# A DRAM scratch array stored chunk by chunk instead of partition by partition

## The chip, the cores and the metric

One core of one Trainium2 chip runs the whole program in one launch. The metric is the device time of that launch in microseconds (us). The unchanged kernel took 11381.7 us as the median of three runs (11377.09 to 11388.17).

## What is computed

64 images of 256x256 pass through a four-layer Fourier network with 32 channels, whose output is one value a pixel. Each row of the output image is a token of width 256; 77 text tokens are appended, and a transformer layer (attention and a routed feed-forward) follows. All is in float32.

```python
v = h @ p_w + p_b                                  # 3 -> 32 channels
for i in range(4):
    x1 = fourier_layer(v, W1, W2)                  # 24 x 12 modes kept
    x2 = einsum('bcxy,cd->bdxy', v, w_w[i]) + w_b[i]
    v = batch_norm(x1 + x2)                        # statistics over all images
    if i < 3: v = relu(v)
out = einsum('bcxy,cu->bxyu', v, q_w) + q_b        # 32 -> 1 channel
h = concatenate([out, txt], axis=1)                # 256 + 77 tokens
h = h + attention(layernorm(h))
h = h + routed_ffn(layernorm(h))
```

The batch norm needs the statistics of all 64 images before any of them can enter the next layer. So the activations of a layer, 64 images x 32 channels x 256 x 256 in float32, are 512 MB, and they lie in DRAM (HBM) between the layers.

## The kernel before

An image's activations are 8 MB and are worked on as 8 chunks, numbered t, of 1 MB each: 128 partitions x 8 rows x 256 values. A chunk's SBUF tile has 8 KB in each partition.

The list `vd` holds two DRAM tiles of 8 MB for each image, one set read and the other written by a layer, in turns. They are declared at line 183. Before the change a tile's dimensions are partition, chunk, row, value.

`layer(i, ...)` (line 526) runs three times, for i = 0, 1, 2. For each chunk of each image:

- `ld` (line 632, in layers 1 and 2 alone) loads the previous layer's chunk into a tile `vin`, of which the pool has four. It does so in two DMAs of 512 KB, each of 4 rows in all partitions (line 636).
- `pre` (line 656) makes the new values in PSUM with TensorE: the inverse Fourier part from `y`, and in layers 1 and 2 the 32x32 channel mix of `vin` (line 673).
- `evA` and `evB` (lines 685 and 687) apply the relu and write the tile `vo`, of which there are four, by ScalarE or VectorE.
- `st` (line 691) stores `vo` to DRAM in two DMAs of 512 KB (line 694).
- `turn` (VectorE transpose, line 699), `prod` and `sq` (lines 710 and 721: the mix for the next layer's variance, squared by ScalarE), `y` (line 732: the forward Fourier part) use the same `vo`.

Layer 0 has no `ld`: it builds its input from the raw image, which GpSimd loads. The order of all steps within an image is written out by hand in two strings (`ORDER`, one for layer 0 and one for layers 1 and 2), in which `@1` or `@2` means the step belongs to one or two images later. So instructions stand on every engine in that fixed order.

All loads and stores of activations are issued by SyncE (SP), in program order, on one DMA queue. The DMAs of this queue use eight completion semaphores in rotation, and the program has each of them wait for the DMA eight before it, besides the wait for its data or its buffer. For instance, the first half of a store waits for the eighth DMA back and for ScalarE.

The mixing of modes (`mix`, line 410) runs between the layers. It needs all images' spectra and works on no activation.

The last layer's activation is never stored. `image_rows(b)` (line 942) reads the third layer's chunks again as tiles `ch`, 1 MB in one DMA each (line 962), and contracts the 32 channels to one with TensorE (line 964). There are seven `ch` buffers. `attention` and `feed_forward` then work on the tokens, and the loads run up to two images ahead of them.

Of the kernel before, what the change touches and what calls it, by code (L numbers as in the profile page):

```python
# [9 lines left out]
F32 = mybir.dt.float32  # L10
# [6 lines left out]
S = 256  # L17
# [136 lines left out]
def tile_fno_fusion_transformer(ctx: ExitStack, tc: tile.TileContext, a, cst_d, grid_d, out):  # L154
    nc = tc.nc
    x = a["x"].rearrange("b x y o -> b x (y o)")
    B = x.shape[0]
# [4 lines left out]
    dram = ctx.enter_context(tc.tile_pool(name="dram", bufs=1, space=DRAM))  # L162
# [17 lines left out]
    epsc = const.tile([128, 1], F32, name="epsc")  # L180
    nc.vector.memset(epsc, EPS)

    vd = [dram.tile([128, 8, 8, S], F32, name=f"v{b}_{n}") for n in range(2) for b in range(B)]
    vd = [vd[:B], vd[B:]]
    mix_d = [dram.tile([B, 2, KX, 32 * C], F32, name=f"mix{i}") for i in range(L)]
    xh_d = [dram.tile([128, B, 144], F32, name=f"xh{i}") for i in range(1, L)]
# [3 lines left out]
    def evict(dst, src, act_every=3):  # L190

        flip[0] += 1
        if act_every and flip[0] % act_every == 0:
            nc.scalar.copy(dst, src)
        else:
            nc.vector.tensor_copy(dst, src)
# [329 lines left out]
    def layer(i, st, src, dst, acc):  # L526
# [7 lines left out]
        with ExitStack() as cx:  # L534
# [64 lines left out]
            y_, t32, vin, vo, half_, zts = {}, {}, {}, {}, {}, {}  # L599
# [32 lines left out]
            def ld(b, t, e):  # L632
                vin[b, t] = ip.tile([128, 8, S], F32, name="vin")
                for n in range(2):
                    rows = slice(4 * n, 4 * n + 4)
                    nc.sync.dma_start(vin[b, t][:, rows], src[b][:, t, rows])

            def sp(b, h, e):
                ps = take(("sp", b, h), 1)[0]
# [51 lines left out]
            def st_(b, t, e):  # L691
                for n in range(2):
                    rows = slice(4 * n, 4 * n + 4)
                    nc.sync.dma_start(dst[b][:, t, rows], vo[b, t][:, rows])

            def turn(b, t, e):
                if (b, t // 2) not in t32:
# [84 lines left out]
            def xs(b, n, e):  # L782
                nc.sync.dma_start(xh_d[i][:, b, :], xos.pop(b).rearrange("p g k -> p (g k)"))

            run = dict(
                am=am, lx=lx, ld=ld, sp=sp, spT=spT, pre=pre, evA=ev(0), evB=ev(1), st=st_, turn=turn,
                prod=prod, sqA=sq(0), sqB=sq(1), y=y, half=half, zt0=zt(0), zt1=zt(1), x=x_, xo=xo, xs=xs,
            )
            steps = []
            for word in ORDER[min(i, 1)].split():  # L790
                word, _, late = word.partition("@")
                word, _, e = word.partition(".")
                name = word if word in run else word.rstrip("0123456789")
# [50 lines left out]
    src = vd[L % 2]  # L844
# [87 lines left out]
    rows = [128, 128, TXT]  # L932
# [6 lines left out]
    def psum():  # L939
        return pp.tile([128, 512], F32, name="pp")  # L940

    def image_rows(b):
        am = ap_.tile([2 * KX, 32 * C], F32, name="am")
        nc.sync.dma_start(am, mix_d[L - 1][b].rearrange("p k c -> (p k) c"))
        tmp = am.rearrange("p (o k) -> p o k", k=32)
        nc.vector.tensor_tensor(
            tmp, tmp, qrow[0:2 * KX].to_broadcast([2 * KX, C, 32]), ALU.mult
        )
        a1 = ap_.tile([2 * KX, 32], F32, name="a1")
        nc.vector.reduce_sum(a1, tmp.rearrange("p o k -> p k o"), axis=AX.X)  # L950
        ps = psum()
        nc.tensor.matmul(ps[0:32, 0:S], lhsT=a1, rhs=EXT[0:2 * KX], start=True, stop=True)
        y1 = ap_.tile([32, 2, 128], F32, name="y1")
        evict(y1.rearrange("k t p -> k (t p)"), ps[0:32, 0:S], 2)
        hp = pb_.tile([128, 2, S], F32, name="hp")
        for t in range(2):
            nc.tensor.matmul(  # L957
                hp[:, t, :], lhsT=y1[:, t, :], rhs=T4[0:32], start=t == 0, stop=False, skip_group_check=True
            )
        for t in range(8):  # L960
            ch = inp.tile([128, 4, 2, S], F32, name="ch")
            nc.sync.dma_start(ch.rearrange("p g r y -> p (g r) y"), src[b][:, t])
            for g in range(4):
                nc.tensor.matmul(  # L964
                    hp[32 * g:32 * g + 32], lhsT=win[:, 7 - t:39 - t], rhs=ch[:, g], start=False, stop=t == 7,
                    skip_group_check=True,
                )
        h = tp.tile([128, 3, D], F32, name="h")
        nc.scalar.activation(h[:, 0:2, :], hp, AF.Identity, bias=hbias, scale=1.0)  # L969
        nc.sync.dma_start(h[0:TXT, 2, :], a["txt"][b])  # L970
        return h
# [131 lines left out]
    def feed_forward(b, h1, z, fw, place):  # L1103
# [65 lines left out]
        nc.gpsimd.dma_start(out[b, S:TOK], o[0:TXT, 2, :])  # L1169

    hs = {n: image_rows(n) for n in range(min(2, B))}
    done = attention(hs.pop(0))
    done += select(done[1])
    for b in range(B):
        now = done
        if b + 2 < B:
            hs[b + 2] = image_rows(b + 2)
        if b + 1 < B:
            done = attention(hs.pop(b + 1))
        feed_forward(b, *now)  # L1180
        if b + 1 < B:
            done += select(done[1])
# [33 lines left out]
```

## Time and profile before

| what | value |
|---|---|
| median of three runs | 11381.7 us |
| the profiled execution's own time | 11393.82 us |
| its span, first to last instruction | 11392.0 us |
| TensorE (PE) busy | 10594.2 us |
| VectorE (DVE) busy | 8460.5 us |
| ScalarE (ACT) busy | 6496.0 us |
| GpSimd (POOL) busy | 1477.9 us |
| read from HBM / written to it | 1761.87 MB / 1696.92 MB |

The profiled execution lies 12.1 us above the median, 0.1%. A page of this profile shows the busy share of each engine in 40 slices of the span, the share of the 16 DMA engines in use, and the bytes that they moved. By the times at which lines run, the program has these stages: first transform and mix (to about 300 us), layer 0 (to about 2300 us), mix (to about 2680 us), layer 1 (to about 5450 us), mix (to about 5800 us), layer 2 (to about 8600 us), mix and weight preparation (to about 8790 us), then contraction, attention and feed-forward of the 64 images.

A matmul's end in this profile is modelled and matmuls overlap, so a high PE share doesn't say that PE is at its peak. The share of the DMA engines is the sum of the durations of their packets over 16 times the stretch. The trace also has every single packet, with its start, duration and size.

### The profile page before, as it was taken

The numbers are of one execution on the slowest core, as the hardware profiler recorded it, in microseconds if no ns is written. First come the engines' busy times: TensorE is split into PE (matmuls) and PEld (weight loads), VectorE is DVE, ScalarE is ACT, GpSimd is POOL, SyncE is SP. The second block draws the span as 40 slices with busy tenths as digits, with TensorE's granted clock in tenths as the row PEclk, the third lists the DMA queues.
The fourth block names the chain that finished last, engine by engine and source line by source line (L and its number), as shares of the span: only waits on it lengthen the run. The fifth ranks groups of instructions, "written<-read, shape, count | busy, mean of one in ns | idle before, by whom it ended". The sixth has DMA issues, their size and how long they took to land. (4 is left out here: it accounts for less than half of the span.)

```text
span 11392.0 us, 408517 instructions
## 1 busy us (share of the span) xinstructions
PE 10594.2 (93%) x182038; PEld 5729.6 (50%) x182038; DVE 8460.5 (74%) x10405; ACT 6496.0 (57%) x10697; POOL 1477.9 (13%) x2243
## 2 busy tenths in 40 slices
PE   6999999997999999999699999999995999999998
PEld 3555555543444444444344444444443666666666
DVE  5888888886777777777677777777775666666665
ACT  5777777775656655665556566565653333333333
POOL 0111111110000000000100000000001333333333
PEclk7999999998999999999899999999997999999999
DMA  7776676769999999999899999999998555555553
GB/s 233 248 248 244 247 250 246 248 238 326 378 383 376 383 379 375 376 380 380 296 374 383 379 383 380 377 373 371 382 376 279 224 222 224 228 230 227 229 227 135
DMA packets 977151, 3485.52 MB, mean 306 GB/s; under 512 B 151320, under 2 KB 200856, under 8 KB 905368
## 3 DMA queue, kind: packets, MB, share of 16 engines
q1 hardware_dynamic: 906880, 3376.23, 77.5%
q0 software_dynamic: 61360, 79.44, 3.1%
q8 instruction: 1424, 23.33, 0.8%
q10 hardware_dynamic: 7144, 3.72, 0.1%
q14 instruction: 343, 2.81, 0.1%
HBM read 1761.87 MB, written 1696.92 MB: 304 GB/s over the span
## 5 line engine op out<-in xcount | busy, mean ns | idle before, releaser
L721 ACT ACTIVATE ring<-ring 128x1024 f32<-128x1024 f32 x3072 | 3115.8, 1014 | 1182.0 <-PE ring L710 1116.4
L699 DVE STREAM_TRANSPOSE t<-vo 128x2048 f32<-128x2048 f32 x1536 | 3465.1, 2286 | 20.5 <-DVE vo L687 0.5
L710 PE MATMUL ring<-vo,w 32*32 32x512 f32 x49152 | 2411.8, 600 | 85.8 <-ACT vo L685 71.0
L687 DVE TENSOR_SCALAR vo<-ring 128x1024 f32<-128x1024 f32 x1280 | 1544.7, 1221 | 1195.4 <-PE ring L673 806.4
L685 ACT ACTIVATE vo<-ring 128x1024 f32<-128x1024 f32 x1792 | 1792.0, 1023 | 1043.3 <-PE ring L673 494.5
L732 PE MATMUL ring<-t,cst 32*32 32x512 f32 x49152 | 2072.6, 599 | 47.1 <-issue 40.8
L732 PEld LDWEIGHTS ring<-t,cst 32*32 32x32 f32 x49152 | 911.6, 103 | 924.9 <-issue 617.6
L710 PEld LDWEIGHTS ring<-vo,w 32*32 32x32 f32 x49152 | 802.2, 103 | 1071.6 <-issue 398.9
L611 POOL TENSOR_TENSOR ams<-ams,bns 48x512 f32<-48x512 f32 x384 | 401.4, 1045 | 6980.6 <-DMA ams<-mix 6710.2
L662 PE MATMUL ring<-cst,y 24*128 24x256 f32 x16384 | 1228.0, 402 | 76.2 <-DVE vo L687 58.2
L673 PE MATMUL ring<-vin,ws 32*32 32x512 f32 x32768 | 1281.2, 602 | 18.6 <-issue 13.2
L662 PEld LDWEIGHTS ring<-cst,y 24*128 24x128 f32 x16384 | 787.6, 185 | 989.7 <-DVE vo L687 389.0
L650 DVE STREAM_TRANSPOSE y<-ring 128x1024 f32<-128x1024 f32 x384 | 762.9, 1987 | 327.1 <-PE ring L642 326.2
L662 PE MATMUL ring<-mv,y 29*128 29x256 f32 x8192 | 703.8, 404 | 36.6 <-ACT ring L721 19.7
L662 PEld LDWEIGHTS ring<-mv,y 29*128 29x128 f32 x8192 | 455.2, 185 | 368.8 <-ACT ring L721 211.3
L766 PEld LDWEIGHTS ring<-cst,zt 128*128 128x128 f32 x4608 | 533.2, 193 | 178.3 <-ACT vo L685 114.3
L742 ACT COPY half<-ring 128x1024 f32<-128x1024 f32 x192 | 194.4, 1013 | 727.2 <-PE ring L732 727.1
L1165 POOL DMA_DIRECT2D out_dram<-o x1024 | 510.9, 507 | 660.6 <-DVE o L1160 617.6
L721 ACT ACTIVATION_READ_ACCUMULATOR ring<-ring 128x1 f32 x3072 | 584.9, 190 | 0.0
L766 PE MATMUL ring<-cst,zt 128*128 128x96 f32 x4608 | 565.3, 279 | 7.9 <-DVE zt L750 7.3
L750 DVE STREAM_TRANSPOSE zt<-ring 128x1024 f32<-128x1024 f32 x192 | 377.0, 1963 | 244.6 <-PE ring L732 244.6
L642 PE MATMUL ring<-ams,cst 49*128 49x512 f32 (+1 forms) x1536 | 450.3, 642 | 104.9 <-POOL ams L611 38.4
(367 smaller groups left out, 9812.4 us busy)
## 6 DMA issues: line engine op xcount, KB each, us to landing
v<-vo SPq DMA_DIRECT2D x3072, 512.0 KB, 7.9
vin<-v SPq DMA_DIRECT2D x2048, 512.0 KB, 9.1
ch<-v SPq DMA_DIRECT2D x512, 1024.0 KB, 12.6
mix<-ob SPq DMA_DIRECT2D x96, 512.0 KB, 5.7
ams<-mix SPq DMA_DIRECT2D x384, 96.0 KB, 8.0
xin<-in_x_dram SPq DMA_DIRECT2D x16, 1024.0 KB, 7.0
mv<-in_x_dram POOLq DMA_DIRECT2D x256, 64.0 KB, 7.5
out_dram<-o POOLq DMA_DIRECT2D x1024, 16.0 KB, 3.0
```

The source lines that it names most:

```text
L642: nc.tensor.matmul(ps[:, n, :], lhsT=EX[hv, 128 * h:128 * h + 128], rhs=ams[b % 2][hv], start=True, stop=True, skip_group_check=True,)
L650: nc.vector.transpose(y_[b, h].rearrange("p q c -> p c q"), ring[key][0][1].rearrange("p n (c k) -> p (n c) k", k=32),)
L662: nc.tensor.matmul(ps[n][:, 256 * r:256 * r + 256], lhsT=y_[b, t // 4][32 * n:32 * n + K, q:q + 4, :].rearrange("p q c -> p (q c)"), rhs=m ...
L673: nc.tensor.matmul(ps[n][32 * j:32 * j + 32], lhsT=ws[32 * n:32 * n + 32], rhs=v[32 * n:32 * n + 32, 2 * j:2 * j + 2, :], start=False, sto ...
L685: nc.scalar.activation(to, ring[key][h][1], AF.Relu)
L687: nc.vector.tensor_scalar(to, ring[key][h][1], 0.0, None, ALU.max)
L699: nc.vector.transpose(t32[b, t // 2][:, :, 8 * (t % 2):8 * (t % 2) + 8, :].rearrange("p y s c -> p s y c"), vo[b, t].rearrange("p s (y l) ...
L710: nc.tensor.matmul(ps[n][32 * j:32 * j + 32], lhsT=w4[i + 1][32 * n:32 * n + 32], rhs=vo[b, t][32 * n:32 * n + 32, 2 * j:2 * j + 2, :], st ...
L721: nc.scalar.activation(ps, ps, AF.Square, accum_out=acc[:, at:at + 1])
L732: nc.tensor.matmul(ps[n][32 * j:32 * j + 32], lhsT=FYT[32 * n:32 * n + 32, k, :], rhs=t32[b, j][32 * n:32 * n + 32, k].rearrange("p s c -> ...
L766: nc.tensor.matmul(ps[:, 0, 96 * g:96 * g + 96], lhsT=zt_[:, h, k0:k0 + 4, :].rearrange("p k c -> p (k c)"), rhs=FX[:, h, 48 * r:48 * r + ...
L1165: nc.gpsimd.dma_start(out[b, 64 * n + 16 * g:64 * n + 16 * g + 16].rearrange("(p t) d -> p t d", t=2), o[32 * g + 8 * n:32 * g + 8 * n + 8 ...
```

## The change

The two outer dimensions of the DRAM tiles are exchanged: chunk, partition, row, value. The three places that index a tile follow.

```diff
-    vd = [dram.tile([128, 8, 8, S], F32, name=f"v{b}_{n}") for n in range(2) for b in range(B)]
+    vd = [dram.tile([8, 128, 8, S], F32, name=f"v{b}_{n}") for n in range(2) for b in range(B)]
...
-                    nc.sync.dma_start(vin[b, t][:, rows], src[b][:, t, rows])
+                    nc.sync.dma_start(vin[b, t][:, rows], src[b][t, :, rows])
...
-                    nc.sync.dma_start(dst[b][:, t, rows], vo[b, t][:, rows])
+                    nc.sync.dma_start(dst[b][t, :, rows], vo[b, t][:, rows])
...
-            nc.sync.dma_start(ch.rearrange("p g r y -> p (g r) y"), src[b][:, t])
+            nc.sync.dma_start(ch.rearrange("p g r y -> p (g r) y"), src[b][t])
```

In bytes: a chunk's partition rows, 8 KB each, lay 64 KB apart in DRAM and spread over the image's 8 MB. Now they lie 8 KB apart, one after the other, and the chunk is one run of 1 MB. A DMA of `ld` or `st` moves 4 KB of each row, so its 128 pieces of 4 KB lay 64 KB apart and now lie 8 KB apart. A DMA of `ch` moves the 8 KB whole. The SBUF side is as it was, and so are the number of DMAs, their order, their sizes and what each waits for: in the built program only the DRAM addresses and strides of 3072 stores and of 2560 loads (2048 `vin`, 512 `ch`) differ.

## The prediction

> **What bounds the kernel now.** I read the page's slices first, to see where DMA could matter at all, since nothing but DRAM addresses changes.
>
> ```profile
> PE   6999999997999999999699999999995999999998
> ...
> DMA  7776676769999999999899999999998555555553
> GB/s 233 248 248 244 247 250 246 248 238 326 378 383 376 383 379 375 376 380 380 296 374 383 379 383 380 377 373 371 382 376 279 224 222 224 228 230 227 229 227 135
> ```
>
> PE is at nine tenths in every long stage. The DMA engines are so in two of them, layers 1 and 2 (slices 10 to 19 and 21 to 30), where each chunk is loaded and stored. Then the stages' inner parts, by windows; columns are busy us (and count) of PE, PEld, DVE, ACT, POOL, then granted clock, DMA share, GB/s:
>
> ```profile
> 3000.00:5400.00 2400.00, 2300.36 (x49127) 1086.07 (x49112) 1803.21 (x1007) 1447.35 (x2279) 109.49 (x105) 1.00 0.98 379
> 5900.00:8500.00 2600.00, 2488.67 (x53167) 1174.84 (x53139) 1951.77 (x1088) 1559.53 (x2456) 121.33 (x116) 1.00 0.98 378
> 400.00:2200.00 1800.00, 1750.58 (x33176) 916.95 (x33144) 1598.22 (x889) 1371.76 (x2170) 214.97 (x299) 1.00 0.70 247
> 8900.00:11100.00 2200.00, 2148.38 (x13131) 1495.85 (x13130) 1487.86 (x5329) 834.43 (x1703) 727.41 (x1265) 1.00 0.58 225
> ```
>
> Rows one and two are layers 1 and 2: the DMA engines 98% in use, PE 95.8% and 95.7%. Row three, layer 0, has PE 97% and DVE 89% busy with DMA at 0.70; row four, the token stage, PE 98% and DMA 0.58. So a faster DMA is worth something in layers 1 and 2 alone, and there PE stands close behind it. Next, the queue in layer 1 (median us from issue to landing is the last figure):
>
> ```profile
> DMA packets 258811, 909.50 MB, mean 379 GB/s; under 512 B 29647, under 2 KB 36431, under 8 KB 258358
> ...
> q1 hardware_dynamic: 258358, 902.65, 97.3%
> ...
> v<-vo SPq DMA_DIRECT2D x848, 512.0 KB, 8.9
> vin<-v SPq DMA_DIRECT2D x845, 512.0 KB, 9.2
> ...
> xh<-xo SPq DMA_DIRECT2D x53, 72.0 KB, 9.0
> ```
>
> 53 images in 2400 us are 45.3 us an image. At 379 GB/s a DMA of 512 KB is 1.4 us of bandwidth, but it lands after 9: about six others are ahead of it, as eight completion semaphores allow. And what SP waits for in that window (us in total, times, longest):
>
> ```profile
> SPq L694 <- ACT vo L685: 431.0, 110, 7.9
> SPq L694 <- DMA v<-vo: 286.2, 314, 2.2
> SPq L694 <- DMA vin<-v: 207.9, 245, 2.5
> SPq L636 <- DMA vin<-v: 189.7, 181, 2.4
> SPq L636 <- DMA v<-vo: 141.5, 158, 1.5
> SPq L603 <- DMA vin<-v: 96.4, 106, 1.7
> SPq L636 <- PE ring L673: 94.1, 73, 2.3
> ```
>
> The five DMA rows are the semaphore rotation, 921.7 us, 38% of the window: DMA sets the pace there. The ACT and PE rows, 525.1 us, 22%, are computation setting it. Neither rules alone.
>
> The packet records say how much slack a packet holds. Of the 216,840 packets of 4 KB that began in 3000 to 5400 us, the fifth percentile, the quartile and the median all took 159 ns, the mean 168.1. So 159 ns is the floor, and 9.1 ns of excess sit in a tail (95th percentile 198, 99th 385). Cut into single microseconds: those that moved 390 GB/s or more, 66% of the stretch, hold 19% of the excess, 1 to 4 ns a packet; those under 350, a fifth of it, hold 62%, 37 to 68 ns a packet. Followed packet by packet, the slow ones stand mostly at restarts. At 4065.7 us most engines ran out of work for 0.5 to 1 us; their next one to three packets took 200 to 800 ns, and then 159 again. That excess follows from a drained queue, and I don't count on the layout to mend it all.
>
> **What the Trainium skill says.** "DMA: Bandwidth & Descriptors", section "Latency and other measured facts", lists copies whose partition rows lie at large power-of-two pitches: 207 GB/s in each direction at 512 KiB, 164 at 2 MiB, 103 at 4 MiB, 214 as the full rate; contiguous tiles are one cure, and aliasing of HBM channels an unverified inference. Our 64 KB pitch is below the list, on its good side. The trace agrees: its best microseconds pass 410 GB/s, about 205 each way. So no collapse is there to be cured. Section "The descriptor swizzle" of the same page gives each DMA engine four neighbouring partitions at a time; engines in step then stand 256 KB apart in DRAM before, 32 KB after. No run here shows it. Section "Where 436 GB/s comes from" puts the ceiling of the 16 ports at 435 GB/s; 4096 bytes in 159 ns by 16 engines are 412, near it, so the floor looks like the engines' own and I leave it at 159.
>
> **The change part by part.** No instruction is added, removed or moved on any engine; waits, queue order and sizes stay, so no queue is passed. A run in DRAM is still 4 KB for `vin` and `vo` and 8 KB for `ch`, so packets keep their number and size. What can change is the time of a packet in HBM.
>
> - Layer 0, 512 MB of stores: mean packet 181 ns in 500 to 2200 us, DMA 0.70. PE and DVE hide it. If stores got 10% slower the share would be 0.77. I take nothing; ends -15 and +20 us, as some waits for a free `vo` stand here too.
> - Token stage, 512 loads of 1 MB: 8 KB packets take 321 ns on average against a floor of 309; DMA 0.58 behind PE at 98%. Nothing; ends -10 and +15 us. If that cover went, `h` (line 969) and the attention after it would come later.
> - Layers 1 and 2. An image has 4096 packets of 4 KB, 256 an engine. Excess: 256 x 9.1 ns = 2.3 us of an image's 45.3, and 128 images have 298 us. That is the whole gain on the DMA side. PE's idle time caps it: (2400 - 2300.4) / 53 = 1.9 us an image, 240 us in all. After that PE is what is late.
>
> For the likeliest value I take a third of the excess, 3 ns a packet, as what belongs to addresses: row neighbours now follow each other in memory, and a part of the tail is in packets far from a restart. That is 0.77 us of DMA an image. Of it I pass on one half, since SP's waits for DMA (38%) and for computation (22%) share the pacing: 0.38 us x 128 = 49 us. Both halvings are choices, not readings. Ends: -240 us (all excess gone, PE cap) and, on the other side, a packet 9 ns dearer, which passes whole as the engines have only 2% left: 256 x 9 ns x 128 = +295 us.
>
> Sum: 11393.8 - 49 = 11345 for the profiled execution; on the median, which stands 12 lower, 11333 us.
>
> **The rivals.** What can be told from no change is 0.2%, 23 us.
>
> 1. A small gain, as summed: 11333 us, chance 0.41, of which some 0.07 is for a gain near the PE cap, 11142 us. For it: a 9 ns tail in a stage at 98% DMA. Against: most of the tail follows drains.
> 2. Nothing to be measured: 11382 us, chance 0.34. For it: three quarters of the packets already take the floor, and the restart explains the tail. A packet has to change by about 0.7 ns passed whole (23 us / 128 / 256), or 1.4 ns passed by half, to be seen.
> 3. Slower: engines in step only 32 KB apart, and successive 4 KB pieces 8 KB apart, meet in the same part of the HBM, within a DMA and between the load and the store streams that now both sweep 1 MB. It would act in layers 1 and 2, in full-rate stretches now at the floor, and pass whole. At 3 ns a packet it costs 256 x 3 ns x 128 = 98 us: 11480 us. It decides from 0.7 ns on. For it: a floor can only be left upwards. Against: small pitches are the good side of the skill's list. Chance 0.25.
>
> That the change doesn't do what it says is ruled out by the built program: the strides differ in 5632 DMAs and nothing else does.
>
> **How the numbers follow.** Faster 0.41, same 0.34, slower 0.25. Predicted 11333. The range, 11200 to 11460, leaves out the gains near the PE cap (about 0.07) and the losses above 2.4 ns a packet, 79 us (about 0.12). The likeliest case's own range is 11200 to 11359.
>
> **What would show it.** Right: in layers 1 and 2 the image's period falls from 45.3 to about 44.9 us, DMA share stays near 0.97 to 0.98 with GB/s about 382, the mean 4 KB packet near 165 ns, and PE's share there rises towards 0.965; layer 0 and the token stage keep their lengths to 15 us. Rival 2: the same table and the same percentiles. Rival 3: the median packet leaves 159 ns, GB/s falls below 376 and SP's waits for DMA grow. I would be wrong altogether if layer 0 or the token stage moved by more than 20 us, or if packets came in another number or size.

## The result and the profile after

The changed kernel took 11480.8 us (median of 4 runs, 11473.5 to 11493.3) against 11383.9 us for the kernel before in the same session: 1.0087 times as long, 95% interval 1.0074 to 1.0100. That is 97 us slower, where 49 us faster was forecast, and outside the range.

First the page's slices of the changed kernel, as shown of before:

```profile
PE   6999999987999999999699999999995999999998
...
DMA  7677666679999999999899999999998555555553
GB/s 234 245 249 248 245 246 249 245 248 330 368 370 379 379 371 370 366 374 372 297 364 379 377 380 372 374 371 372 376 371 280 231 221 221 221 225 230 231 228 133
```

Layer 0 (slices 2 to 9, counted from 1) and the token stage (from 32) move nearly what they moved. In the inner slices of layers 1 and 2 (11 to 19 and 21 to 30) most figures are lower, 364 to 380 where they were 371 to 383. Then the same windows (layer 1, layer 2, layer 0, token stage; columns as before):

```profile
3000.00:5400.00 2400.00, 2274.08 (x48282) 1066.19 (x48258) 1770.65 (x989) 1418.32 (x2236) 108.61 (x104) 1.00 0.99 372
5900.00:8500.00 2600.00, 2481.22 (x52630) 1164.78 (x52636) 1932.61 (x1078) 1544.34 (x2436) 119.08 (x114) 1.00 0.99 375
400.00:2200.00 1800.00, 1751.21 (x33212) 918.52 (x33208) 1600.15 (x889) 1373.57 (x2171) 214.50 (x300) 1.00 0.70 248
8900.00:11100.00 2200.00, 2136.20 (x13022) 1480.68 (x13021) 1489.46 (x5315) 824.05 (x1682) 716.62 (x1248) 1.00 0.58 225
```

In layers 1 and 2 the DMA engines are in use a little more (0.99) and move less (372 and 375 GB/s, before 379 and 378), and PE's share in layer 1 falls from 95.8% to 94.8%. Layer 0 is as it was. In the queue of layer 1 a load now lands after 9.9 us instead of 9.2:

```profile
vin<-v SPq DMA_DIRECT2D x832, 512.0 KB, 9.9
v<-vo SPq DMA_DIRECT2D x832, 512.0 KB, 9.4
```

And SP's waits in that window:

```profile
SPq L694 <- ACT vo L685: 378.0, 105, 8.4
SPq L694 <- DMA v<-vo: 294.5, 314, 2.3
SPq L694 <- DMA vin<-v: 286.5, 257, 2.8
SPq L636 <- DMA vin<-v: 211.4, 221, 2.4
SPq L636 <- DMA v<-vo: 140.4, 156, 2.0
SPq L603 <- DMA vin<-v: 99.0, 104, 2.0
SPq L636 <- PE ring L673: 67.8, 74, 2.2
```

The five DMA rows are 1031.8 us, before 921.7; the ACT and PE rows are 445.8, before 525.1. So the queue sets the pace more often. Most of the growth is in one row, the store that waits for an older load (207.9 to 286.5).

The packet records say why. In the window of layer 1 the 4 KB packet's median is still 159 ns; the mean rose from 168.1 to 171.9, the 99th percentile from 385 to 459 ns (layer 2: 167.9 to 171.5). The single microseconds that moved under 350 GB/s were 20% of the window and are 26%. Laid over each other image by image, the 3rd to 6th microsecond after an image's spectrum is stored (`xh`) had 1 to 2 ns of excess a packet before and have 16 to 52 ns now. About 16 packets are in flight there on average (15.9 to 16.2), so no drained queue shows ahead of this excess. SP issues the load of the next image's chunk 2 at that time, but it lands only some 14 us after the store of `xh`; what is on the engines was issued earlier, by the landing times above all the load of chunk 4. A second such stretch is the two microseconds about the store itself, 2 to 3 ns before and 28 now.

By stages, from the first to the last `xh` store of a layer in the two profiled executions: layer 0 2248 and 2245 us, layer 1 2768 and 2817 (+49), layer 2 2775 and 2806 (+31), the token stage from its first contraction to the end 2619 and 2627 (+8); the rest, mixes and starts, +5. These make up the 90 us between the spans, 11392.0 and 11482.4.

### The profile page after: what moved, and what is told of

The parts are those of the page before. It is cut to its first block, busy times and chain, and to the rows that moved or that the text cites. A ratio compares the mean times of both kernels' runs of the same rounds, so it can differ in the third digit from the quotient of the medians.

```text
span 11482.4 us, 408517 instructions
## 1 busy us (share of the span) xinstructions
PE 10634.4 (93%) x182038; PEld 5732.5 (50%) x182038; DVE 8458.6 (74%) x10405; ACT 6491.1 (57%) x10697; POOL 1473.4 (13%) x2243
## 3 DMA queue, kind: packets, MB, share of 16 engines
q1 hardware_dynamic: 906880, 3376.23, 78.0%
## 5 line engine op out<-in xcount | busy, mean ns | idle before, releaser
L673 PE MATMUL ring<-vin,ws 32*32 32x512 f32 x32768 | 1307.2, 606 | 44.9 <-DMA vin<-v 22.2
```

The source lines that it names most:

```text
L673: nc.tensor.matmul(ps[n][32 * j:32 * j + 32], lhsT=ws[32 * n:32 * n + 32], rhs=v[32 * n:32 * n + 32, 2 * j:2 * j + 2, :], start=False, sto ...
```

## The experiments

All differ from one of the two kernels in the DRAM layout or in how a chunk is cut into DMAs, and were compared with the kernel before on the same chip. This table collects the layouts in which each load and store is two DMAs of 4 KB pieces. Packets are the mean 4 KB packet in layer 1 (3000 to 5400 us) and layer 2 (5900 to 8500 us); layers are from the first to the last `xh` store.

| rows apart by | packet, ns | layer 1 / layer 2, us | time over before (interval) |
|---|---|---|---|
| 64 KB (before) | 168.1 / 167.9 | 2768 / 2775 | 1 |
| 8 KB (after) | 171.9 / 171.5 | 2817 / 2806 | 1.0087 (1.0074 to 1.0100) |
| 4 KB, no holes (e3) | 166.5 / 166.7 | 2748 / 2752 | 0.9963 (0.9950 to 0.9976) |
| 12 KB (e4) | 166.6 / 166.6 | 2746 / 2753 | 0.9963 (0.9950 to 0.9976) |
| 68 KB (e5) | 166.8 / 166.8 | 2747 / 2757 | 0.9956 (0.9940 to 0.9973) |
| 16 KB (e6) | 171.2 / 171.9 | 2798 / 2809 | 1.0062 (1.0047 to 1.0077) |
| 72 KB (e9) | 167.1 / 167.1 | 2748 / 2757 | 0.9966 (0.9953 to 0.9979) |
| 8 KB, halves apart (e12) | 167.6 / 168.2 | 2762 / 2780 | 1.0082 (1.0067 to 1.0097) |
| 32 KB (e13) | 166.8 / 166.9 | 2752 / 2759 | 0.9960 (0.9946 to 0.9974) |

**Loads or stores, or both meeting: e1 and e2.** Layer 1 loads from the first set of tiles and stores to the second, layer 2 the other way round. So giving one set alone the new layout makes four combinations with before and after.

```diff
-    vd = [dram.tile([8, 128, 8, S], ...) ...]
+    vd = [dram.tile([8, 128, 8, S] if n == 1 else [128, 8, 8, S], ...) ...]   # e1; n == 0: e2
```

> Only the second set of DRAM tiles is stored chunk by chunk: layer 1 stores to it and layer 2 loads from it; the first set keeps the old layout. After the full change the mean 4 KB packet rose from 168 to 172 ns in layers 1 and 2 and the time by 97 us. Theory A (the load stream and the store stream meet because both sweep 1 MB runs): no layer has both in the new layout, so 11384 within 25 us, packets 168 ns in both layers. Theory B (the new layout is dearer for loads alone): layer 1 as before, layer 2 as after, 172 ns there, about +45 us. Theory C (dearer for stores alone): layer 1 as after, layer 2 as before, about +50 us.

> Only the first set is stored chunk by chunk: layers 0 and 2 store to it, layer 1 and the token stage load from it. Theory A (streams meet): 11384 within 25 us. Theory B (loads alone): layer 1 at 172 ns a packet, layer 2 at 168, about +50 us. Theory C (stores alone): layer 2 at 172 ns, layer 1 at 168, about +45 us; layer 0 hidden behind PE.

Measured: e1 1.0039 (1.0026 to 1.0052), e2 1.0038 (1.0026 to 1.0051). Layers 1 and 2 of e1, then of e2:

```profile
3000.00:5400.00 2400.00, 2293.27 (x49069) 1084.33 (x49055) 1799.99 (x1006) 1443.97 (x2275) 108.61 (x104) 1.00 0.99 379
5900.00:8500.00 2600.00, 2473.10 (x52730) 1169.31 (x52732) 1935.96 (x1079) 1548.06 (x2444) 119.05 (x114) 1.00 0.99 375
```

```profile
3000.00:5400.00 2400.00, 2280.82 (x48663) 1080.83 (x48632) 1786.54 (x997) 1430.56 (x2253) 108.63 (x104) 1.00 0.99 375
5900.00:8500.00 2600.00, 2483.72 (x53120) 1172.63 (x53104) 1947.15 (x1087) 1562.84 (x2465) 119.07 (x114) 1.00 0.99 378
```

The lower rate, 375, goes with the loads: in layer 2 of e1 and in layer 1 of e2. The new layout for loads alone adds 2.6 ns (layer 1) and 2.4 ns (layer 2) to the mean packet, for stores alone 0.8 and 1.1, for both 3.8 and 3.6. The parts nearly add up, in packets and in time (0.39% and 0.38% of the 0.87%), so theory A, the two streams meeting, falls as the main cause; B is the larger part and C the smaller.

**The pitch of the rows: e3, e4, e5, e6, e9, e13.** The tile's shape is changed and the three places that index it.

```diff
-dram.tile([8, 128, 8, S], ...)
+dram.tile([8, 2, 128, 4, S], ...)   # e3: each half chunk one run of 512 KB
+dram.tile([8, 128, 12, S], ...)     # e4: 12 KB, the last 4 KB unused
+dram.tile([128, 68, S], ...)        # e5: 68 KB, the last 4 KB unused
+dram.tile([4, 128, 16, S], ...)     # e6: 16 KB
+dram.tile([128, 72, S], ...)        # e9: 72 KB, the last 8 KB unused
+dram.tile([2, 128, 32, S], ...)     # e13: 32 KB
```

> Each 512 KB DMA is one run of DRAM (the two halves of a chunk lie one after the other, partition rows 4 KB apart, no holes); the chunk of the token stage is then two 4 KB pieces a partition. Theory holes (a DMA that touches 4 KB of every 8 KB is what costs): back to 11384 or below, packets 168 ns or less. Theory nearness (pieces that are moved at once lie too close): [...]as slow as after or slower, 11480 to 11600, packets 172 ns or more.

> Chunk by chunk with 4 KB left empty behind each partition row: rows 12 KB apart. Theory power of two (rows at 8 KB[...] fall on the same part of the memory): back to 11384 within 25 us, packets 168 ns. Theory nearness: between, 11430 to 11480. Theory streams (both sweep the same span of addresses with the same low bits): unchanged, about 11480, packets 172 ns.

> The old layout, with 4 KB left empty behind each partition row of an image: rows 68 KB apart instead of 64. Theory power of two (what costs is that all 4 KB pieces of one DMA start at the same place of a small power of two, 64 KB or 8 KB): mean 4 KB packet 166.6 ns as with rows of 4 or 12 KB, 11345 us. Theory nearness or image size (what helps at 4 and 12 KB is that a chunk is one region): 168 ns and 11388 us as before.

> Two chunks share a region: rows 16 KB apart, between the 8 KB of after and the 64 KB of before. Theory power of two, with a cost that falls as the pitch grows: 169 to 171 ns, 11400 to 11460 us. Theory that 8 KB alone is bad because the DMA's piece is exactly every second 4 KB: 168 ns or less, 11340 to 11390 us.

> The old layout with 8 KB left empty behind each partition row: rows 72 KB apart, which is no power of two, but the pieces of one DMA all start at an even (or all at an odd) multiple of 4 KB, as with 64, 16 and 8 KB, and unlike 68, 12 and 4 KB. Theory parity (one DMA's pieces keep to one half of an 8 KB interleave): no better than 64 KB, 168 ns or more, 11385 to 11480 us. Theory power of two in the pitch itself: 166.7 ns and 11345 us, as with 68 KB.

> Four chunks share a region: rows 32 KB apart, the missing point between 16 KB (171.5 ns, 11470 us) and 64 KB (168.0 ns, 11390 us). Theory of a cost that falls as the pitch doubles: 169 to 171 ns, 11400 to 11460 us. Theory that 64 KB is special[...]: 171 ns or more, 11460 to 11500.

Layers 1 and 2 with rows 12 KB apart:

```profile
3000.00:5400.00 2400.00, 2315.83 (x49544) 1099.02 (x49528) 1819.22 (x1014) 1461.74 (x2300) 110.73 (x106) 1.00 0.98 382
5900.00:8500.00 2600.00, 2504.15 (x53578) 1191.43 (x53564) 1966.76 (x1098) 1575.32 (x2478) 121.17 (x116) 1.00 0.98 382
```

382 GB/s, and PE at 96.5%, above before. Nearness falls with e3 and e4: pieces 4 and 12 KB apart are the cheapest of all. Parity of the 4 KB block falls with e9, where all pieces of a DMA have the same parity and cost no more than 0.6 ns over the best. A power of two as such falls with e3 and e13, and a cost that shrinks as the pitch doubles falls with e13 as well. The results of e4, e6 and e13 lie outside all the times that were forecast for them. What is left is a pattern without a rule: five layouts share a best value of 166.5 to 167.1 ns, two (8 and 16 KB) cost 4 to 5 ns more, and the old 64 KB about 1.3. So the old layout did have a little to win, 36 to 47 us in these five runs, and the change went to another unlucky pitch.

**Within one DMA, or between the two halves of a chunk: e12.** The pitch inside a DMA stays 8 KB, but the halves are put into regions of their own, so that no other DMA moves the 4 KB between two pieces.

```diff
-dram.tile([8, 128, 8, S], ...)
+dram.tile([8, 2, 128, 8, S], ...)   # half n in [t, n, :, 0:4]
```

> Rows 8 KB apart as in the new layout, but the two halves of a chunk lie in different 1 MB regions, so each DMA's 4 KB pieces have 4 KB of unused memory between them, and no other DMA touches it. Theory within one DMA (pieces at a pitch of 8 KB slow each other, whatever lies between): 171 to 172 ns, 11460 to 11500 us. Theory between the halves (the DMA that moves the other 4 KB of the same rows, in flight beside it, is what is met): 166.6 ns, 11345 us, as with rows of 4 KB.

The time, 11488.8 us, is what the first theory forecast, and read alone it would have misled. The stages say something else: layers 1 and 2 take 2762 and 2780 us, near before, at 167.6 and 168.2 ns; the loss is in the token stage, 2706 us instead of 2619. There one DMA reads a chunk as two pieces of 4 KB a partition, 1 MB apart, and PE waits for it. Of the tile `ch`, what PE waited for and who waited for it (us, times):

```profile
  DMA ch<-v: 190.3, 129
...
  ACT h L969: 672.3, 64
  PEld hp L964: 114.5, 65
  PE hp L964: 75.8, 64
```

PE's wait for `ch` was 27.8 us in the kernel before. The cut into two pieces isn't the reason by itself: e3 reads a chunk as two pieces of 4 KB too, 512 KB apart, and there PE waits 42.4 us for `ch` and the stage takes 2622 us. From 8900 to 11200 us the mean 4 KB packet takes 168.8 ns in e3 and 176.2 ns in e12. So something in e12's addresses costs in this stage although no DMA moves what lies between the pieces: the 8 KB between rows, or the 1 MB between the halves that one DMA reads. Which of them isn't shown.

For layers 1 and 2 the second theory holds in the main: with the halves apart, 4.3 and 3.3 of the 5.3 and 4.9 ns that 8 KB cost over 12 KB are gone. Why interleaved halves cost at 8 and 16 KB and not at 12 or 32 isn't shown.

**Pieces of 8 KB: e7, e8, e10, e11.** If two interleaved DMAs are the matter, a chunk moved by one DMA should not care about the layout.

```diff
-                for n in range(2):
-                    rows = slice(4 * n, 4 * n + 4)
-                    nc.sync.dma_start(vin[b, t][:, rows], src[b][t, :, rows])
+                nc.sync.dma_start(vin[b, t], src[b][t])        # e8, e10: loads (e7: [:, t]; e11: [t, :, 0:8])
...
+                nc.sync.dma_start(dst[b][t], vo[b, t])         # e8: stores too (e7: [:, t])
```

> The old layout, but each chunk's load and each chunk's store is one DMA of 1 MB instead of two of 512 KB: pieces of 8 KB, rows 64 KB apart. An 8 KB packet's floor is 309 ns against 2 x 159. If DMA time of the queue sets layers 1 and 2: 256 x 4.5 ns = 1.15 us less an image, half passed on, about 11310 us. If the later start of a store (it now waits for both halves) sets it: 11390 to 11450.

> The new layout with one DMA of 1 MB a chunk: one contiguous run, no 4 KB left out between pieces. Theory that pieces of 4 KB at every second place are what costs in the new layout: the loss goes, and it equals the old layout with 1 MB DMAs within 25 us or is faster. Theory that neighbouring rows or meeting streams cost: 60 to 100 us slower than the old layout with 1 MB DMAs.

> The new layout; loads of 1 MB in one DMA (8 KB pieces without holes), stores left as two DMAs of 4 KB pieces. If the loads' 4 KB pieces carry most of the loss (of 3.7 ns a packet the loads' layout gave about 2.6, the stores' about 0.9): within 40 us of the next run, which differs in the row pitch alone, and below 11430. If the stores carry it: 60 us or more above the next run.

> Rows 12 KB apart, loads of 1 MB in one DMA, stores as two DMAs. 8 KB packets have a floor of 309 ns against 2 x 159, so the loads need 128 x 9 ns = 1.15 us an image and engine less. If layers 1 and 2 still follow the DMA engines: 11250 to 11310. If what computes sets the pace once packets are at 166.6 ns, or if a load of 1 MB holds up the store behind it: 11340 to 11400.

Loads and stores of 1 MB: 1.0068 (1.0053 to 1.0083) in the old layout and 1.0078 (1.0063 to 1.0093) in the new. The mean 8 KB packet in layer 1 is 326.5 and 326.2 ns: the layouts no longer differ. Both lose for the other reason expected, and more than was forecast for e7 (11476.4 us, forecast 11390 to 11450). SP's waits in layer 1 of e7 show it (its store now waits for the whole chunk's eviction, and DMA is hardly waited for):

```profile
SPq L690 <- DVE vo L685: 1429.9, 316, 14.8
SPq L634 <- PE ring L671: 342.1, 134, 5.3
SPq L634 <- PE ring L706: 47.2, 47, 1.6
SPq L690 <- DMA v<-vo: 46.9, 44, 1.6
```

Most of that loss is in layer 0, 2311 us instead of 2248. With loads alone in 1 MB, e10 takes 11422.7 us and e11 11383.5. Their load packets are equal (333.8 and 333.9 ns); their stores, still in halves, take 166.2 and 164.0 ns, which is 128 x 2.2 ns x 128 images = 36 us, if it passes whole, of the 39 between them (the forecast for the loads' case was within 40). So the whole-chunk load takes the loads' share of the loss away and the stores' share stays. The hope for a faster kernel from fewer packets failed: 333.9 ns is more than twice 159, and e11 is no faster than before (0.9994, 0.9985 to 1.0003).

**Loads split by partitions: e14 and e15.**

```diff
-                    nc.sync.dma_start(vin[b, t][:, rows], src[b][t, :, rows])
+                    half = slice(64 * n, 64 * n + 64)
+                    nc.sync.dma_start(vin[b, t][half], src[b][t, half])
```

> The new layout, rows 8 KB apart; each load is split by partitions (64 partitions of 8 KB, 512 KB in one run) instead of by rows, the stores are as they were. With rows 8 KB apart but the two halves in regions of their own, layers 1 and 2 ran at 168 ns (2762 and 2780 us from first to last image, before 2768 and 2775, after 2817 and 2806). Theory between the halves (two DMAs in flight that interleave in the same 1 MB): the loads no longer interleave, so layers 1 and 2 take 2740 to 2790 us. Theory within one DMA or of the region's density: 2800 us or more. A DMA of 64 partitions that spreads worse over the DMA engines would also show above 2800, with fewer bytes a second.

> Rows 12 KB apart, loads split by partitions. No theory has a cost left in this layout, so it is the reference for the run before and a candidate: 8 KB packets of loads have a floor of 309 ns against 2 x 159, at most 1.15 us less an image and engine. If that is passed on: 11250 to 11330 us. If the packets' excess grows as it did with loads of 1 MB (334 ns): 11340 to 11400.

Both are 12% slower (1.1162, 1.1143 to 1.1181, and 1.1170, 1.1152 to 1.1188). The window 3200 to 6000 us of e14:

```profile
3200.00:6000.00 2800.00, 2483.45 (x47028) 1103.91 (x47033) 1726.35 (x963) 1391.78 (x2187) 104.44 (x100) 0.93 1.00 311
```

The DMA engines are in use all the time and move 311 GB/s. The 8 KB packets, all loads, have a median of 547 ns (556 in e15) where 309 is the floor. Layers 1 and 2 of e14 take 3365 and 3439 us: of its forecasts the last came true, fewer bytes a second, and e15 is far from both of its own. This bound hides any layout, so the pair decides nothing about it.

## Why the prediction was wrong

- **Where it can act.** Right. Layers 1 and 2 hold 80 of the 90 us; layer 0 moved by 3, the token stage by 8. (The 181 ns given for layer 0 mixes in GpSimd's image loads; the stores alone take 177 ns there.)
- **Packets in number and size.** Right, 906880 packets on the queue before and after.
- **The step that failed** is the choice of sign: "For the likeliest value I take a third of the excess, 3 ns a packet, as what belongs to addresses: row neighbours now follow each other in memory". Three or so nanoseconds do hang on addresses, but they were added (3.8 and 3.6). Of the old layout's 9.1 ns only about 1.4 belonged to the addresses, as the best layouts show; the rest stays in all of them. How much of that belongs to restarts, to which the prediction gave most of it, isn't shown: in layer 1 before, packets that start after a microsecond with at least 15 packets always in flight hold 55% of the excess. The restart put at 4065.7 us stands at 4055.3 us in the time of the views, and at 4063.4 us, 7 us after it, packets take up to 915 ns without a drain ahead of them.
- **What led there** is the argument against rival 3, "small pitches are the good side of the skill's list". The Trainium skill, "DMA: Bandwidth & Descriptors", section "Latency and other measured facts", lists pitches from 512 KiB up, moved in pieces of 16 KiB, and recommends contiguous tiles or a pad of a few KiB. I read it as a curve that goes on downwards. The runs agree on the pad (68 KB beats 64 by 0.44%) and on contiguity where the whole run is one DMA (e3, 4 KB). They differ for a contiguous chunk that two DMAs move in alternate 4 KB: the measurement decides.
- **How much passes.** One half was taken. A loss of 3.8 and 3.6 ns is 0.97 and 0.92 us an image (256 packets an engine), 62 and 59 us in 64 images; 49 and 31 arrived, two thirds. A gain of 1.5 and 1.3 ns (e4) is 25 and 21 us, and 22 and 22 arrived, all of it.
- **Rival 3** gave the price and the time, 3 ns and 11480 us; 3.7 ns and 11481 were measured. That the time fits so closely is luck: 3 ns were taken to pass whole, while of 3.7 ns 80 us of 121 arrived, and 10 us came from the other stages. Its mechanism was half right. The load and the store stream meeting isn't it (e1, e2), and the median packet kept 159 ns. But part of the loss does fall in stretches that ran at the floor before, in episodes and not throughout, on the loads more than on the stores, and by e8 and e12 it is in the main tied to the two halves of a chunk in flight together; e12's token stage leaves a part open. It had a chance of 0.25 and a price near the range's edge, and the range stopped at 2.4 ns without a reading that excluded more.

## What to carry to other kernels

Where DMA engines are in use 98% of a stage, the layout in DRAM is a tuning parameter with both signs, here from 0.4% faster to 0.9% slower. It has to be measured at several pitches, because contiguous isn't best by itself: by these runs it also matters how the run is cut into DMAs that are in flight together. The two cheap cures here are equal, one contiguous run for each DMA (e3) or a pad of 4 KB behind each row (e4, e5): 0.9963 and 0.9956 to 0.9963 of the time before; e9 and e13 can't be told from them. And a whole time can hide two effects: in e12 only the stages showed that the loss had moved, and only e3 showed that the two pieces were not enough to explain it.

## What was not expected of the hardware

- The cost of a row pitch isn't monotonic: 4, 12, 32, 68 and 72 KB take 166.5 to 167.1 ns for a 4 KB packet, 64 KB 168, 8 and 16 KB 171 to 172.
- A load into 64 partitions ran its 8 KB packets at a median of 547 ns instead of 309, and the whole stage at 311 GB/s with the engines in use 100%. The Trainium skill, "DMA: Bandwidth & Descriptors", section "Rules for kernel authors", advises against two transfers to disjoint partition halves because they share the same engines; here they also cost 1.8 times the packet time.
- A DMA share near 1 says little of the rate: it was 0.98 at 382 GB/s, 0.99 at 372 and 1.00 at 311.
